# Reading the expert tables in a step of their own, spreading the token turns to one a half, and moving the late expert tiles

## The chip, the cores and the metric

The kernel runs on one core of a Trainium2 chip. Time is device microseconds (us) of one execution; the figure to be explained is the median of several. One execution was also taken with the hardware profiler; it has a time of its own, which differs a little from the median.

The core has five engines that work side by side, each with its own instruction queue: TensorE (PE in the profile, PEld for its weight loads), VectorE (DVE), ScalarE (ACT), GpSimd (POOL) and SyncE (SP). DMAs are issued from an engine's queue and land later.

## The reference, cut to what matters

```
x                                   # 4 batches x 2048 tokens x 512
xn  = layernorm(x)
q,k,v = split(xn @ w_qkv)           # 16 heads of 32
q,k = spectral_filter(q), spectral_filter(k)   # rfft, mask, irfft along the 32
out = softmax(q k^T / sqrt(32)) v @ w_out + b_out
moe: best = argmax(softmax(xn @ w_gate))       # 8 experts, top 1
     the first 100 tokens of each expert, in order over all 8192 tokens:
     gate * (xn @ w_expert + b_expert), else 0  # one w_expert for all
return x + out + moe
```

At most 800 tokens get an expert's output. They are the 800 *slots*, kept as 7 tiles of 128 rows, called expert rows 0 to 6 here.

## The kernel before, in words

**Groups, blocks, windows, halves.** Everything is float32. The work is cut into 16 *groups*, each one batch with 4 of its 16 heads (`k`; batch `k // 4`, head group `c = k % 4`). A group has four *blocks* of 512 queries (`n`). A block goes over 16 key tiles of 128 (`j`). One key tile of one block is a *half*; a *window* is two halves, an even and an odd one. Halves are numbered through the program, 0 to 1023, 64 to a group and 16 to a block; a window is named here by its first half ("window 824").

In a half, TensorE computes the scores of 4 heads (keys x queries, 512 columns), and, between them, two *maxima* products of a block 21 halves ahead (queries x keys; VectorE reduces them, `part<-array`, to row maxima, which must be known before the exponentials, because the softmax subtracts them). ScalarE takes the exponentials of the scores into a tile of 128 x 2048 called `even` or `odd`, in two instructions of 1024 columns (`even<-array`, `odd<-array`). TensorE multiplies the tile of the half before with `v`, and VectorE adds that to `num`. After an even and an odd half, the odd tile is added onto the even one by an accumulating DMA of 1 MB from GpSimd's queue (`pair`: `even<-odd`), issued one window later; two windows later GpSimd adds the last window's even tile to this one in two instructions of 128 x 1024 (`add_to`, here "the sums": `even<-even`). So one even tile collects a block's denominators. There are five buffers for `even` and three for `odd`; an exponential waits when its buffer isn't free.

**Closing a block.** `close_steps(k, n)` lists the steps for the block that ended last, by halves after its end: *fold* (5: row sums by a product with ones), *invert* (6 to 13: eight reciprocals of 64 columns on VectorE), *divide* (on GpSimd, at the 14th half), *result* (17 to 20: the output projection of 128 tokens each, copied to `y`), *add* (21: `out_dram<-y`, an accumulating DMA of 1 MB from GpSimd's queue). For the last block but one (`(k, n) == (15, 2)`) they lie closer: fold at 5, inverts at 6 to 8, divide at 9, results from 10, add at 14.

**Pieces.** The keys, queries and values of the next group are computed in the halves of this one, in *pieces* of 128 tokens. There are three kinds: QK with `s = 0`, QK with `s = 1`, and V. Each piece has a first and a last half (`release`, `stop`), and a small planner, `level`, puts each in a half that has little cost yet. "QK3.3" is the last 128 tokens of the fourth 512.

**Turning groups.** Groups 3, 7 and 11 are the last of their batch; there the next batch's tokens are prepared. For each of the 16 token tiles, ScalarE *normalises* it (`normalize`, in the half before, in place), and TensorE *turns* it (`turn`: four transposes, then ScalarE copies the result to `xnT`). `TURNS` says in which half of the group each tile is turned; a piece can only be computed behind the turn of its own tile. Later in the same group the tokens' experts are found (`follow_route`), and each token's number and gate are sent by indirect DMAs to four tables of slots (`table<-entry,slot`). In the last batch the same is done in group 11, and the tables are read in group 12, the first group of the last batch.

**Expert rows.** `expert_steps` has the steps and `place_experts` their halves, written out by hand:

- `begin` (half 804): loads of `w_expert` and `b_expert`, the loads of the four tables (`entries<-table`, SyncE's queue), the reduction of these to one (`entry`, `who`: two VectorE reductions and a copy), a GpSimd memset of the first row buffer;
- `clear_rest`: the memset of the second one;
- `fetch(i)`: gathers row tile `i` from `x` by an indirect DMA from GpSimd's queue;
- `measure(i)`: mean and variance of the row tile on VectorE;
- `scale`: for all seven rows together, GpSimd computes `rstd` and `shift`;
- `expert(i)`: ScalarE normalises row `i` with `rstd` and `shift` (`xg<-xg,shift,rstd`); in the same step row `i-1` is turned and row `i-2` multiplied with the weights, for rows 0 to 3;
- for rows 4 to 6, the *late tiles*, `turn_row` and four `expert_columns` (128 output columns each) are placed in the last group by `LATE`: the first number of each tuple is the half of the turn, the others the halves of the columns, counted from half 960;
- `gather_row(i)`, `add_row(i)`, `scatter_row(i)`, two halves apart: gather the rows from the output by an indirect DMA, add on GpSimd, and scatter them back by an indirect DMA. All of them, and `out_dram<-y`, write to or read the same output and so wait for the landing of the one before.

**What sets the order.** Nothing reorders at run time: VectorE, ScalarE, GpSimd and TensorE are kept in program order (`InOrder`, whose line 83 records every operation, so all rows of the profile name L83). In a window the order is: the split of the maxima, the steps in `heads` (divide), `pair`, `add_to`, then for each of the two halves the scores, maxima, exponentials and their reductions, the product with `v`, and last `agenda[half]` with all steps placed there (steps placed by `behind` come last). An engine that stands before an instruction holds all that is behind it.

PSUM has eight banks. Banks 0 to 3 hold the scores; class `Oldest` hands out 4 to 7 for the maxima and for everything else that needs one.

Of the kernel before, what the change touches and what calls it, by code (L numbers as in the profile page):

```python
# [12 lines left out]
F32 = mybir.dt.float32  # L13
# [8 lines left out]
B, S, DM = 4, 2048, 512  # L22
# [3 lines left out]
P = 128  # L26
NT = S // P
NR = DM // P
# [4 lines left out]
TQ = QB // P  # L33
SLOTS = E * CAP
ST = -(-SLOTS // P)
EARLY = 4
LATE = ((14, 15, 16, 22, 23), (24, 25, 26, 27, 28), (29, 30, 31, 32, 38))
NTAB = 4
FAR = 1 << 20
EPS = 1e-5  # L40
# [62 lines left out]
def attention_and_top1_experts(ctx: ExitStack, tc: tile.TileContext, a: dict, out: bass.AP):  # L103
# [56 lines left out]
    small = ctx.enter_context(tc.tile_pool(name="small", bufs=1))  # L160

    def chunk(name):
        tag, bufs = ("y", 1) if name == "y" else ("xs", None)
        return chunks.tile([P, TQ, DM], F32, tag=tag, name=name, bufs=bufs)
# [28 lines left out]
    on = SimpleNamespace()  # L193
# [367 lines left out]
    def expert_steps():  # L561


        def begin():
            w_exp = chunk("w_exp")
            on.sync.dma_start(out=w_exp, in_=a["L0_ffn_w_expert"].rearrange("(r p) n -> p r n", p=P))
            b_exp = work.tile([P, DM], F32, tag="b_exp", name="b_exp", bufs=1)
            on.sync.dma_start(out=b_exp, in_=a["L0_ffn_b_expert"].partition_broadcast(P))
            entries = small.tile([P, NTAB, ST, 2], F32, name="entries")
            for i, table in enumerate(tables):  # L570
                on.sync.dma_start(out=entries[:, i], in_=table.rearrange("(t p) c -> p t c", p=P))
            entry = small.tile([P, ST, 2], F32, name="entry1")
            for i, op in enumerate((ALU.min, ALU.max)):
                on.vector.tensor_reduce(
                    entry[:, :, i], entries[:, :, :, i].rearrange("p n t -> p t n"), AX.X, op
                )
            who = small.tile([P, ST], I32, name="who")
            on.vector.tensor_copy(who, entry[:, :, 0])
            xg = [chunk("xg"), small.tile([P, ST - TQ, DM], F32, name="xg1")]
            on.gpsimd.memset(xg[0], 0.0)  # L580
            mv = small.tile([P, ST, 2], F32, name="mv1")
            index = [bass.IndirectOffsetOnAxis(ap=who[:, i : i + 1], axis=0) for i in range(ST)]
            bound = {"bounds_check": B * S - 1, "oob_is_err": False}
            taken.update(mv=mv, w_exp=w_exp, b_exp=b_exp, entry=entry, index=index, bound=bound, xg=xg)

        def clear_rest():
            on.gpsimd.memset(taken["xg"][1], 0.0)

        def row(i):
            return taken["xg"][i // TQ][:, i % TQ, :]  # L590

        def fetch(i):
            on.gpsimd.indirect_dma_start(row(i), None, rows, taken["index"][i], **taken["bound"])

        def measure(i):
            stats = small.tile([P, 6], F32, name="stats1")
            on.vector.bn_stats(stats, row(i))
            on.vector.bn_aggr(taken["mv"][:, i, :], stats)

        def scale():  # L600
            rstd = small.tile([P, ST], F32, name="rstd1")
            on.gpsimd.tensor_scalar(rstd, taken["mv"][:, :, 1], EPS, None, ALU.add)
            on.gpsimd.tensor_tensor(rstd, rstd, power[:, 0:ST], ALU.pow)
            shift = small.tile([P, ST], F32, name="shift1")
            on.gpsimd.tensor_tensor(shift, taken["mv"][:, :, 0], rstd, ALU.mult)
            on.gpsimd.tensor_scalar(shift, shift, -1.0, None, ALU.mult)
            taken.update(rstd=rstd, shift=shift)

        def turn_row(i):
            px = bank()  # L610
            for r in range(NR):
                on.tensor.transpose(px[:, r * P : (r + 1) * P], row(i)[:, r * P : (r + 1) * P], ident)
            taken["xt"] = work.tile([P, QB], F32, tag="byx", name="xt", bufs=1)
            on.scalar.copy(taken["xt"], px)

        def expert_columns(i, q):
            cols = slice(q * P, (q + 1) * P)
            pe = bank()[:, cols]
            for r in range(NR):
                columns(  # L620
                    pe,
                    taken["xt"][:, r * P : (r + 1) * P],
                    taken["w_exp"][:, r, cols],
                    start=(r == 0),
                    stop=(r == NR - 1),
                )
            on.vector.tensor_tensor(row(i)[:, cols], pe, taken["b_exp"][:, cols], ALU.add)
            if q == NR - 1:
                on.scalar.activation(row(i), row(i), AF.Copy, scale=taken["entry"][:, i : i + 1, 1])

        def expert(i):

            if 2 <= i < EARLY + 2:
                at = slice(i - 2, i - 1)
                pe = bank()
                for r in range(NR):
                    on.tensor.matmul(
                        pe,
                        lhsT=taken["xt"][:, r * P : (r + 1) * P],
                        rhs=taken["w_exp"][:, r, :],  # L640
                        start=(r == 0),
                        stop=(r == NR - 1),
                    )
                on.vector.tensor_tensor(row(i - 2), pe, taken["b_exp"], ALU.add)
            if 1 <= i <= EARLY:
                turn_row(i - 1)
            if 2 <= i < EARLY + 2:
                on.scalar.activation(row(i - 2), row(i - 2), AF.Copy, scale=taken["entry"][:, at, 1])
            if i < ST:
                at = slice(i, i + 1)  # L650
                on.scalar.activation(
                    row(i), row(i), AF.Identity, bias=taken["shift"][:, at], scale=taken["rstd"][:, at]
                )

        return clear_rest, begin, fetch, measure, scale, expert, turn_row, expert_columns

    def gather_row(i):
        if i < EARLY:
# [290 lines left out]
    def at(half, step, *args, cost=0):  # L949
        agenda[half].append(lambda: step(*args))  # L950
        costs[half] += cost
# [73 lines left out]
    def place_experts(start):  # L1025


        clear_rest, begin, fetch, measure, scale, expert, turn_row, expert_columns = expert_steps()
        first = start + 36
        at(first, begin)  # L1030
        at(first + 5, clear_rest)
        for i in range(ST):
            at(first + 2 + 2 * i, fetch, i)
            at(start + (46, 47, 48, 53, 55, 56, 57)[i], measure, i)
        at(first + 22, scale)
        for i in range(ST):
            at(first + 26 + 2 * i, expert, i, cost=(NR if 2 <= i < EARLY + 2 else 0) + (1 if 1 <= i <= EARLY else 0))
        tail = start + 3 * GH
        for i, (turned, *places) in enumerate(LATE):
            at(tail + turned, turn_row, EARLY + i, cost=0.5)  # L1040
            for q, half in enumerate(places):
                at(tail + half, expert_columns, EARLY + i, q, cost=1)
        for i in range(ST):
            free = start + GH + i * HB + 26 if i < EARLY else tail + (25, 30, 39)[i - EARLY]
            for step in (gather_row, add_row, scatter_row):
                at(free, step, i)
                free += 2

    def plan(k):
# [43 lines left out]
        for s in range(3):  # L1093
            mine = [piece for piece, kind in zip(pieces, kinds) if kind == s]
            for i, piece in enumerate(mine):
                n = i // TQ
                if s == 0:
                    stop = start + GH - MAX_AHEAD // 2 - 1 + n * HB
                    release = start + 1 + n * HB
                elif s == 1:  # L1100
                    release = start + SPENT + n * TQ
                    stop = release + 3 * TQ - 2
                else:
                    release, stop = start + 1, start + GH + i - 2
                if c == NG - 2 and b + 1 < B:
                    stop = min(stop, start + GH - (8 if s == 2 else 1))
                release = max(release, turned.get(i, start - 1) + 1)
                load = None
                if i == NT - 1 and k + 2 < B * NG:
                    load = lambda s=s: load_qkv_weights(k + 2, s)  # L1110
                jobs[s].append((release, stop, 0 if i else 5 + (k < 2), piece, load))
        for n in range(NQ):
            at(start + GH - 10 + n * TQ, key_steps, n)

    TURNS = (2, 4, 6, 6, 6, 7, 7, 8, 12, 12, 12, 13, 16, 19, 21, 22)
    SPENT = GH - HB - MAX_AHEAD // 2 + TQ
    ROUTE = len(first_route)
    assert ROUTE == 12 + NT + 1
# [174 lines left out]
```

## Time and profile before

| | |
|---|---|
| median of 3 runs | 4135.46 us (4131.81 to 4139.23) |
| profiled execution, its own time | 4130.4 us |
| its span in the profile | 4128.6 us |
| TensorE (PE) busy | 4105.5 us, 99% of the span |
| VectorE (DVE) busy | 3418.3 us, 83% |
| GpSimd (POOL) busy | 3015.6 us, 73% |
| ScalarE (ACT) busy | 2486.1 us, 60% |
| DMAs issued by software (GpSimd's) | 601.63 MB, 74.7% of 16 DMA engines |
| `even<-odd`, 1 MB each | 504, median 8.3 us from issue to landing |
| `out_dram<-y`, 1 MB each | 63, median 9.9 us from issue to landing |

The span is the stretch that the profiler saw; the 1.8 us beyond it lie around the program. A row of a group or timeline names the engine, the operation and `out<-in` by the program's names, with the shape as partitions x elements; behind the bar, or in brackets, stands the idle time of the engine just before and what ended it. In a table by windows each cell is the busy time with its number of instructions, for PE, PEld, DVE, ACT, POOL and SP in turn; behind them the granted clock of TensorE (1.00 is full speed), the share of the DMA engines, and what they moved in GB/s.

Share of busy time in 40 slices of the span, in tenths:

```profile
PE   9999999999999999999999999999999999999999
DVE  7888887978888888797888888888788888888885
ACT  4555565676655556567665556566666555665665
POOL 1678776776887777676787766767678777786787
```

### The profile page before, as it was taken

To read this page: it belongs to the slowest core of one execution; us is meant where nothing else is said; L and a number is where in the kernel's file an instruction comes from. 1 tells how busy PE (TensorE), PEld (TensorE's weight loads), DVE (VectorE), ACT (ScalarE), POOL (GpSimd) and SP (SyncE) were. 2 spreads that over 40 slices of the span, in tenths; PEclk is the share of its full clock that TensorE was granted. 3 is DMA by queue.
4 is the path that set the end of the run, shared out by engine and by line. 5 is a ranking of instruction groups with operands and counts; after the bars stand their busy time and mean duration, and the time that the engine had idled before them with its cause. 6 is when DMAs were issued, how large, how long until landed. Compare 5 with 4: busy or idle time off the path is not lost.

```text
span 4128.6 us, 122052 instructions
## 1 busy us (share of the span) xinstructions
PE 4105.5 (99%) x53184; PEld 1832.0 (44%) x53184; DVE 3418.3 (83%) x4876; ACT 2486.1 (60%) x3424; POOL 3015.6 (73%) x2122
## 2 busy tenths in 40 slices
PE   9999999999999999999999999999999999999999
PEld 5444445444444444444444444444444444444442
DVE  7888887978888888797888888888788888888885
ACT  4555565676655556567665556566666555665665
POOL 1678776776887777676787766767678777786787
PEclk9999999999999999999999999999999999999999
DMA  4787887987788878899788788789887887877877
GB/s 127 147 165 154 160 165 160 226 186 147 154 161 162 163 155 161 188 203 193 145 158 160 158 161 160 159 191 208 171 160 151 173 163 150 170 163 156 163 152 147
DMA packets 179488, 680.81 MB, mean 165 GB/s; under 512 B 23478, under 2 KB 54360, under 8 KB 114184
## 3 DMA queue, kind: packets, MB, share of 16 engines
q0 software_dynamic: 109856, 601.63, 74.7%
q1 hardware_dynamic: 69024, 71.34, 5.3%
q8 instruction: 416, 6.82, 0.6%
q14 instruction: 120, 0.98, 0.1%
q10 hardware_dynamic: 72, 0.03, 0.0%
HBM read 71.07 MB, written 87.91 MB: 39 GB/s over the span
## 4 chain that ended last, share of the span: by engine, by line
PE 97%; DVE 1%; DMA 1%; POOL 0%; issue 0%; ACT 0%; SPq 0%; POOLq 0%; ACTq 0%; DVEq 0%
PE array L83 97%; DVE part L83 1%; POOL even L83 0%; DMA even<-odd 0%; DMA entries<-table 0%; DMA odd<-in_L_attn_w_qkv_dram 0%; ACT xs L83 0%; DVE num L83 0%; ACT xnT L83 0%; DVE factor L83 0%; DMA table<-entry,slot 0%; DVE stats L83 0%; POOL out_dram L83 0%; ACT odd L83 0%; POOL rest L83 0%
## 5 line engine op out<-in xcount | busy, mean ns | idle before, releaser
L83 DVE TENSOR_REDUCE part<-array 128x1 f32<-128x512 f32 (+1 forms) x3066 | 2480.7, 865 | 630.4 <-PE array L83 625.4
L83 POOL TENSOR_TENSOR even<-even 128x1024 f32<-128x1024 f32 x876 | 2123.9, 2527 | 466.7 <-DMA even<-odd 465.8
L83 PE MATMUL array<-keys,q 32*128 32x512 f32 x8192 | 2040.9, 613 | 2.5 <-ACT keys L83 0.8
L83 PE MATMUL array<-q,steps_of_keys 32*128 32x512 f32 x8128 | 2009.7, 614 | 0.2
L83 ACT ACTIVATE odd<-array 128x1024 f32<-128x1024 f32 x1024 | 994.7, 1021 | 462.5 <-PE array L83 388.0
L83 ACT ACTIVATE even<-array 128x1024 f32<-128x1024 f32 x1014 | 983.7, 1021 | 417.8 <-PE array L83 409.5
L83 PEld LDWEIGHTS array<-keys,q 32*128 32x128 f32 x8192 | 760.1, 184 | 540.7 <-DVE part L83 326.7
L83 PEld LDWEIGHTS array<-q,steps_of_keys 32*128 32x128 f32 x8128 | 690.4, 183 | 243.4 <-issue 227.0
L83 DVE TENSOR_TENSOR num<-num,array 128x512 f32<-128x512 f32 x960 | 651.0, 678 | 37.7 <-PE array L83 37.7
L83 POOL DMA_DIRECT2D even<-odd x504 | 462.4, 917 | 277.1 <-ACT odd L83 235.6
L83 PEld LDWEIGHTS array<-xnT,w 128*32 128x32 f32 x16384 | 460.0, 110 | 286.3 <-DVE part L83 196.0
L83 PE MATMUL array<-odd,v 128*32 128x512 f32 x4096 | 546.3, 605 | 0.5 <-DVE part L83 0.5
L83 PE MATMUL array<-even,v 128*32 128x512 f32 x4056 | 540.1, 605 | 3.3 <-DVE part L83 3.3
L83 PE MATMUL array<-xnT,w 128*32 128x128 f32 x16384 | 534.7, 273 | 1.1 <-ACT xnT L83 1.0
L83 PEld LDWEIGHTS array<-w,xnT 128*32 128x32 f32 x8192 | 231.5, 110 | 144.6 <-DVE part L83 100.3
L83 DVE RECIPROCAL factor<-den 128x64 f32<-128x64 f32 x504 | 274.7, 546 | 0.0
L83 PE MATMUL array<-w,xnT 128*32 128x128 f32 x8192 | 267.9, 273 | 0.1
L83 PE MATMUL array<-wo,ot 128*32 128x512 f32 x2048 | 266.7, 593 | 0.0
L83 PEld LDWEIGHTS array<-odd,v 128*32 128x32 f32 x4096 | 80.7, 108 | 388.6 <-DVE part L83 380.6
L83 PEld LDWEIGHTS array<-even,v 128*32 128x32 f32 x4056 | 79.8, 108 | 387.9 <-DVE part L83 383.4
L83 POOL DMA_DIRECT2D out_dram<-y x63 | 87.4, 1387 | 156.3 <-ACT y L83 112.1
L83 ACT COPY keys<-array 128x128 f32<-128x128 f32 x256 | 68.2, 266 | 176.8 <-PE array L83 172.3
(152 smaller groups left out, 1540.5 us busy)
## 6 DMA issues: line engine op xcount, KB each, us to landing
even<-odd POOLq DMA_DIRECT2D x504, 1024.0 KB, 8.3
out_dram<-y POOLq DMA_DIRECT2D x63, 1024.0 KB, 9.9
xs<-in_L_attn_x_dram SPq DMA_DIRECT2D x96, 256.0 KB
out_dram<-in_L_attn_x_dram SPq DMA_DIRECT2D x16, 1024.0 KB
w<-wd SPq DMA_DIRECT2D x30, 256.0 KB
w<-in_L_attn_w_qkv_dram SPq DMA_DIRECT2D x16, 256.0 KB
wo<-in_L_attn_w_out_dram SPq DMA_DIRECT2D x16, 256.0 KB
negm<-row SPq DMA_DIRECT2D x192, 4.0 KB
```

The source lines that it names most:

```text
L83: done = act(*args, **kwargs)
```

## The change

Three things are changed, all in where steps stand; no instruction is added or removed.

1. *Turns.* `TURNS` no longer has two or three turns in one half; each of the 16 tiles has a half of its own. The last half allowed for the QK pieces of the group ahead of a turning group goes from the last half of that group (`start + GH - 1`) to the first half of the turning group (`start + GH`). By the planner, the one piece that this moves there is QK3.3, from half 191 to half 192 (and alike in the two other turning groups); the pieces that wait for a turn move with the turns.
2. *Tables.* The reduction of the tables is taken out of `begin` into a step of its own, `read_tables`, five halves behind it. The steps behind it move: fetches from halves 806, 808, ... 818 to 810, 811, 813, 814, 816, 817, 819; measures from 814, 815, 816, 821, 823, 824, 825 to 814, 816, 821, 823, 825, 827, 829; `clear_rest` from 809 to 806; `scale` from 826 to 830; `expert(i)` from 830 + 2i to 831 + 2i.
3. *Late tiles.* The turns of rows 4, 5, 6 move from halves 974, 984, 989 to 973, 982, 987; their columns to the halves right behind these, but for row 4's last one, which moves to 982; the last columns of row 6 from half 998 to 991. The gather, sum and scatter go from 985, 987, 989 to 984, 986, 988 (row 4), from 990, 992, 994 to 988, 990, 992 (row 5), and from 999, 1001, 1003 to 993, 995, 997 (row 6). The last of these, `scatter_row(6)`, now stands in half 997, right behind the `out_dram<-y` of the block that ended at half 976.

```diff
-LATE = ((14, 15, 16, 22, 23), (24, 25, 26, 27, 28), (29, 30, 31, 32, 38))
+LATE = ((13, 14, 15, 16, 22), (22, 23, 24, 25, 26), (27, 28, 29, 30, 31))
...
             for i, table in enumerate(tables):
                 on.sync.dma_start(out=entries[:, i], in_=table.rearrange("(t p) c -> p t c", p=P))
+            xg = [chunk("xg"), small.tile([P, ST - TQ, DM], F32, name="xg1")]
+            on.gpsimd.memset(xg[0], 0.0)
+            mv = small.tile([P, ST, 2], F32, name="mv1")
+            taken.update(mv=mv, w_exp=w_exp, b_exp=b_exp, entries=entries, xg=xg)
+
+        def read_tables():
+            entries = taken["entries"]
             entry = small.tile([P, ST, 2], F32, name="entry1")
             for i, op in enumerate((ALU.min, ALU.max)):
                 on.vector.tensor_reduce(
...
             who = small.tile([P, ST], I32, name="who")
             on.vector.tensor_copy(who, entry[:, :, 0])
-            xg = [chunk("xg"), small.tile([P, ST - TQ, DM], F32, name="xg1")]
-            on.gpsimd.memset(xg[0], 0.0)
-            mv = small.tile([P, ST, 2], F32, name="mv1")
...
         first = start + 36
         at(first, begin)
-        at(first + 5, clear_rest)
+        at(first + 2, clear_rest)
+        at(first + 5, read_tables)
         for i in range(ST):
-            at(first + 2 + 2 * i, fetch, i)
-            at(start + (46, 47, 48, 53, 55, 56, 57)[i], measure, i)
-        at(first + 22, scale)
+            at(first + 6 + 3 * i // 2, fetch, i)
+            at(start + (46, 48, 53, 55, 57, 59, 61)[i], measure, i)
+        at(first + 26, scale)
         for i in range(ST):
-            at(first + 26 + 2 * i, expert, i, cost=...)
+            at(first + 27 + 2 * i, expert, i, cost=...)
...
-            free = start + GH + i * HB + 26 if i < EARLY else tail + (25, 30, 39)[i - EARLY]
+            free = start + GH + i * HB + 26 if i < EARLY else tail + (24, 28, 33)[i - EARLY]
...
                 if c == NG - 2 and b + 1 < B:
-                    stop = min(stop, start + GH - (8 if s == 2 else 1))
+                    stop = min(stop, start + GH - (8 if s == 2 else 0))
...
-    TURNS = (2, 4, 6, 6, 6, 7, 7, 8, 12, 12, 12, 13, 16, 19, 21, 22)
+    TURNS = (2, 4, 6, 7, 8, 9, 10, 12, 13, 14, 15, 16, 18, 20, 21, 22)
```

More of the change, by code (lines that the diff above doesn't have):

```diff
@@ L578, in begin @@
             on.vector.tensor_copy(who, entry[:, :, 0])
-            xg = [chunk("xg"), small.tile([P, ST - TQ, DM], F32, name="xg1")]
-            on.gpsimd.memset(xg[0], 0.0)
-            mv = small.tile([P, ST, 2], F32, name="mv1")
             index = [bass.IndirectOffsetOnAxis(ap=who[:, i : i + 1], axis=0) for i in range(ST)]
             bound = {"bounds_check": B * S - 1, "oob_is_err": False}
-            taken.update(mv=mv, w_exp=w_exp, b_exp=b_exp, entry=entry, index=index, bound=bound, xg=xg)
+            taken.update(entry=entry, index=index, bound=bound)
         def clear_rest():
@@ L653, in expert @@
                 )
-        return clear_rest, begin, fetch, measure, scale, expert, turn_row, expert_columns
+        return begin, clear_rest, read_tables, fetch, measure, scale, expert, turn_row, expert_columns
     def gather_row(i):
@@ L1025, in place_experts @@
     def place_experts(start):
-        clear_rest, begin, fetch, measure, scale, expert, turn_row, expert_columns = expert_steps()
+        begin, clear_rest, read_tables, fetch, measure, scale, expert, turn_row, expert_columns = expert_steps()
         first = start + 36
         at(first, begin)
-        at(first + 5, clear_rest)
+        at(first + 2, clear_rest)
+        at(first + 5, read_tables)
         for i in range(ST):
-            at(first + 2 + 2 * i, fetch, i)
-            at(start + (46, 47, 48, 53, 55, 56, 57)[i], measure, i)
-        at(first + 22, scale)
+            at(first + 6 + 3 * i // 2, fetch, i)
+            at(start + (46, 48, 53, 55, 57, 59, 61)[i], measure, i)
+        at(first + 26, scale)
         for i in range(ST):
-            at(first + 26 + 2 * i, expert, i, cost=(NR if 2 <= i < EARLY + 2 else 0) + (1 if 1 <= i <= EARLY else 0))
+            at(first + 27 + 2 * i, expert, i, cost=(NR if 2 <= i < EARLY + 2 else 0) + (1 if 1 <= i <= EARLY else 0))
         tail = start + 3 * GH
```

## The prediction

> **What bounds the kernel.** First the page's head and its shares of the chain that ended last.
>
> ```profile
> span 4128.6 us, 122052 instructions
> ...
> PE 97%; DVE 1%; DMA 1%; POOL 0%; issue 0%; ACT 0%; SPq 0%; POOLq 0%; ACTq 0%; DVEq 0%
> ```
>
> TensorE is the bound, and the change removes no matmul, so only waits of TensorE can come or go. To find them I cut the trace into halves: matmuls stand in program order, a float32 matmul leaves two records and a transpose one, so counting records gives each half's first matmul, and a half lasts from its start to the next. A half without a step takes 2.91 us, a projection piece or a result adds 0.88, a turned tile 0.59; nearly all halves fit. What is over that is a wait.
>
> Next the chain in order of time, at the expert tables, and the granted clock by windows.
>
> ```profile
> 3260.72 2.17 DMA table<-entry,slot
> ...
> 3262.90 7.88 DMA entries<-table
> ...
> 3272.03 68.20 PE array L83 x858
> ```
>
> ```profile
> 3266.79:3273.88 7.09, 4.03 (x36) 1.31 (x32) 3.90 (x9) 1.98 (x2) 4.75 (x5) 1.00 1.09 187
> ...
> 4072.80:4076.20 3.40, 3.40 (x18) 0.59 (x16) 0.69 (x1) 1.99 (x3) 0.77 (x1) 0.50 1.02 274
> ```
>
> VectorE stands before the reduction of the tables until they land, and the maxima behind it hold TensorE: half 805 takes 7.09 us, where its like take 3.94. The column after POOL is the clock: 1.00 over that gap (3.06 us idle), 0.50 for 3.4 us late in the last block.
>
> Then the timelines of GpSimd, where the steps of the change queue, and of ScalarE, which waits for it: start, duration, instruction, and in brackets the idle time before it and what ended that.
>
> ```profile
> 3351.81 4.68 POOL L83 TENSOR_TENSOR even<-even 128x1024 f32<-128x1024 f32 x2 [3.92 <-DMA even<-odd]
> 3356.44 0.85 POOL L83 DMA_DIRECT2D even<-odd  x1
> 3357.03 4.96 POOL L83 TENSOR_TENSOR even<-even 128x1024 f32<-128x1024 f32 x2
> 3362.09 0.26 POOL L83 TENSOR_SCALAR rstd<-mv 128x7 f32<-128x7 f32 x1
> ...
> 3364.33 0.28 POOL L83 TENSOR_SCALAR shift<-shift 128x7 f32<-128x7 f32 x1
> ...
> 4028.86 1.31 POOL L83 DMA_DIRECT2D out_dram<-y  x1 [1.59 <-ACT y L83]
> ...
> 4030.90 0.91 POOL L83 DMA_DIRECT2D even<-odd  x1
> 4034.53 4.67 POOL L83 TENSOR_TENSOR even<-even 128x1024 f32<-128x1024 f32 x2 [2.73 <-DMA even<-odd]
> 4040.78 1.10 POOL L83 DMA_INDIRECT w<-out_dram,who  x1 [1.58 <-DMA out_dram<-y]
> ```
>
> ```profile
> 3369.96 0.81 ACT L83 ACTIVATE xg<-xg,shift,rstd 128x512 f32<-128x512 f32 x1
> ...
> 4057.59 1.94 ACT L83 ACTIVATE even<-array 128x1024 f32<-128x1024 f32 x2 [1.14 <-POOL even L83]
> ...
> 4070.04 1.94 ACT L83 ACTIVATE odd<-array 128x1024 f32<-128x1024 f32 x2 [4.27 <-DMA even<-odd]
> ```
>
> GpSimd works far behind the program: `scale`, issued in half 826 (start 3351.09), ends at 3364.61, 13.5 us later. ScalarE's first use came at 3369.96, so that was free. At the end, exponentials wait for GpSimd's sums or its DMAs to give their buffers back.
>
> **The parts.** The sum is made against the profiled execution, 4130.4 us (span 4128.6), 5.1 under the median of 4135.46; the difference is carried to the median.
>
> *Turns.* In a turning group the waits over the fit are 0.52, 0.18, 0.18, 0.48, 0.63, 0.55, 0.18, 0.18 (halves 1, 3, 5, 7, 8, 13, 20, 22): 2.9 us. The 0.48, 0.63 and 0.55 follow halves in which two or three turns and as many normalisations queue on ScalarE. With one of each, ScalarE has 2.04 (exponentials) + 0.59 + 0.81 + 0.27 = 3.7 us of work in a half of 4.39, and the four halves that already hold one piece and one turn (8, 13, 16, 22) delay nothing behind them. The 0.52 follows a half 0 without a piece, and the last query piece now fills it. A turn beside a result or a fold still costs its 0.18, now five times: 0.9. Saved 2.0 a group, three groups: -6.0. The pieces moved by this cost the same 0.88 where they land, and weights still have five halves (19 us) to arrive.
>
> *Tables.* The reduction goes five halves on, to 809, about 18 us; the entries land at 3270.8, before it. 7.09 becomes 3.94: -3.15. The memset (1.40 us) and the fetches only change place on GpSimd; a fetch lands 3.4 to 4.6 us after its issue, and `measure` follows by four halves or more (15 us), so that even 10 us of lag on GpSimd is covered. The reduction's three instructions (0.2 us each, started 0.1 apart) end on VectorE before the next maxima are there: 0.
>
> *Measures.* One behind a reciprocal costs 0.33 (halves 824 to 826, at 4.11 to 4.13 instead of 3.80). Three become four, one of them with some slack: +0.15.
>
> *Scale and the first expert row.* `scale` goes from 826 to 830, but the row that needs it only from 830 to 831. In the changed kernel's order ScalarE has: exponentials of 831, row 0 (waits for the shift on GpSimd), the copy of piece V3.3, the exponentials of 832. On GpSimd I follow the rows: the sums of window 824 start 9.5 us into half 824, when their DMA lands (before: 3351.81, 9.0 in); then sums 4.7 twice, key step 1.2, split 1.5, sums 4.9, division 1.3, sums 4.7, `scale` 2.5, DMA issues and their waits 2, together 27.5. Half 830 starts 23.8 after half 824, so `scale` ends at 830 + 13.2. ScalarE reaches row 0 at 830 + 7.3 and stands 6 us. Behind it stands V3.3, whose bank the second maxima of half 832 need at 830 + 9.2; row 0 (0.8) and the copy (0.27) end at 14.2. TensorE waits 5.0 us. If GpSimd came 3 us sooner it would be 2, if 3 later 8. A gap of 2.31 us inside a stretch of 3.4 was followed by 0.50 for 3.4 us, while 3.06 us at the tables was not. 5 us lies beyond both, so I take one such stretch, 1.7 us (bounds 0 and 3.4): +6.7. The skill's "TensorE: Matmul & The Clock Gate", Part 1, has a free-running window of about 3.4 us, over which an idle array drops to half rate; by it the drop is nearly certain and the part is +6.7, and without any drop it is +5.0.
>
> *Expert rows.* Odd halves instead of even: a result drained late by VectorE now meets a turn (half 834, up to 0.8), other places swap: +0.6 (0 to 1.5).
>
> *Late tiles.* Their columns are drained by VectorE after a reciprocal, 0.17 each, more where a turn shares the half. Before 2.0 us over halves 973 to 997; after, more of them in halves with a reciprocal, and half 992 empty: 2.75. +0.75 (0 to 2).
>
> *The last scatter.* Each `scatter_row` and `gather_row` waits for the landing of the write to `out` before it, and GpSimd stands meanwhile. Before, `gather_row(6)` waited thus for `out_dram<-y`, with one DMA and two sums run in between (4030.90 to 4039.2). After, `gather_row(5)` and `gather_row(6)` stand right behind a scatter (1.7 us each, from its landing of 2.8), which with row 6's own gather and sum (2.4) makes GpSimd 5.5 us later by half 997; and `scatter_row(6)` stands right behind that `out_dram<-y`, whose landing took 11.7 us here and 13.5 at 3333.32, just behind another DMA, as it will be. From half 998's start: `out_dram<-y` issued at 2.0, landed 15.5, the DMA of window 998 issued at 17.3 (before: -0.2), sums of 998 done at 22.7. The exponential of 1002 needs that buffer at 14.6, so it waits 8. The queue then runs on DMA (7.6) and sums (4.7): windows 1000, 1002, 1004 issue at 23.3, 30.3, 37.4. Before, the last of these was at 29.3, and the two waits behind it (4070.04, 4075.82) hung on it. They come 8.1 later, with 0.88 less work in between, since row 6's last columns left half 998: +8.9. With the shorter landing it is +7; bounds +4 and +11. The skill's "DMA: Bandwidth & Descriptors", Anatomy of one DMA, gives 2.0 us + bytes/436e3, an estimate of 4.4 us for this 1 MB; by it GpSimd would stand 9 us less and this part be about 0, the whole sum -1. The rows of the same transfer, 11.7 and 13.5, go against it.
>
> Sum: -6.0 - 3.15 + 0.15 + 6.7 + 0.6 + 0.75 + 8.9 = +7.95. On the median 4143.4, on the profiled execution 4138.4. Its own range, with the bounds but not all at one end: 4137 to 4150.
>
> **Rivals.**
> 1. *GpSimd is early enough at both places*, because with its steps spread it no longer lags, so neither new wait reaches TensorE. For: exponentials have five even and three odd buffers, 8 to 15 us of cover, and row 6's work has left the end of the queue, which would bring the last DMA 2 us forward. Against: 13.5 us of lag at `scale`, and a wait written into the queue. -6.0 - 3.15 + 1.5 - 2 = -9.6: 4126. It decides if `scale` ends within 7 us of half 830.
> 2. *One of the two alone*: -1 or +1, 4135 to 4137.
> 3. *The lateness piles up*: GpSimd reaches both places some 3 us later than I reckon (the missing pause at 805 gives it 3.15 us less to catch up), and each stall drops the clock twice: +3 at `scale`, +1.7, +2 at the end, 4150.
> 4. *The turns save nothing*, if a half with piece, turn and normalisation is as slow as the present 8 and 13: then +14, in with the third.
>
> **Numbers.** The forecast lies at the edge of 0.2% (8.3 us, about what a measurement of this kernel can tell from no change); I give its upper side more, since a wait that empties TensorE makes others late and none of the bounds runs as far down. Forecast 0.55 (0.33 slower, 0.22 same), rival 2 0.11 (same), rivals 3 and 4 0.19 (slower), rival 1 0.15 (faster): faster 0.15, same 0.33, slower 0.52. 4128 to 4151 leaves out most of the first and the end of the third.
>
> **What would show it.** Right: half 805 at 3.9 us; no half of a turning group over its work by more than 0.2; `xg<-xg,shift,rstd` on ScalarE with a wait of about 6 us put down to GpSimd, and a gap of 5 on TensorE; the indirect `out_dram<-xg` behind the last but one `out_dram<-y` of GpSimd waiting some 12 us, then an `even<-array` waiting about 8. Wrong: `scale` done before 830 + 7, a scatter that waits under 4 us, or turning groups that keep their 2.9 us.

## The result and the profile after

The changed kernel takes 4143.49 us (median of 15 runs, 4141.23 to 4146.85), the kernel before beside it 4138.09: a ratio of 1.0017, with a 95% interval of 1.0011 to 1.0024. By that ratio it is 7 us slower (4.5 to 9.9), against the 8 that the prediction had; the two medians themselves lie 5.4 us apart. In a later set, beside another set of runs of the kernel before, it was 1.0023 (1.0014 to 1.0032).

The profiled execution took 4145.56 us, 15.2 more than the profiled one of before, which is more than twice what the ratio gives. The two profiles must therefore not simply be subtracted; where the rest comes from is shown further below. The head of the page and its shares of the chain of waits:

```profile
span 4143.8 us, 122054 instructions
...
PE 97%; POOL 1%; DMA 1%; DVE 0%; issue 0%; ACT 0%; SPq 0%; POOLq 0%; ACTq 0%
```

In the chain GpSimd (POOL) has come up from 0% to 1%, since waits for it have come, and VectorE (DVE) has gone from 1% to 0%. The shares are too coarse to show the wait for the tables, which was 3 us; the table below shows that it is gone. The two instructions more than before are not TensorE's: there are four more waits for semaphores and two fewer reductions of the maxima.

The table by windows, for half 805 first, and then for the two stretches in which TensorE's clock was halved (columns as before: PE, PEld, DVE, ACT, POOL, then the clock):

```profile
3269.03:3272.99 3.96, 3.96 (x36) 1.28 (x32) 3.79 (x6) 1.98 (x2) 3.36 (x4) 1.00 1.11 198
...
3378.60:3385.40 6.80, 5.14 (x42) 2.23 (x46) 1.92 (x2) 2.92 (x4) 6.69 (x6) 0.50 0.62 130
...
4061.25:4068.05 6.80, 4.13 (x16) 1.36 (x17) 0.00 (x0) 3.88 (x4) 6.74 (x5) 0.50 0.85 172
```

Half 805 lasts 3.96 us, with TensorE busy throughout. The two stretches at 0.50 lie in halves 832 and 1002 to 1003, the two places that the prediction named, and each is 6.8 us long.

At the first place, GpSimd's timeline, then ScalarE's:

```profile
3371.59 4.99 POOL L83 TENSOR_TENSOR even<-even 128x1024 f32<-128x1024 f32 x2
3376.67 0.26 POOL L83 TENSOR_SCALAR rstd<-mv 128x7 f32<-128x7 f32 x1
...
3378.92 0.29 POOL L83 TENSOR_SCALAR shift<-shift 128x7 f32<-128x7 f32 x1
```

```profile
3379.24 0.81 ACT L83 ACTIVATE xg<-xg,shift,rstd 128x512 f32<-128x512 f32 x1 [4.85 <-POOL shift L83]
```

Half 830, in which the program has `scale`, began at 3367.03. GpSimd finished it at 3379.21, 12.2 us later (13.2 had been reckoned), and expert row 0 on ScalarE stood 4.85 us for it (6 had been reckoned). Half 832 took 10.72 us instead of 3.9.

TensorE's timeline has a gap at each of the two places, at the first behind ScalarE's copy `v`, which stands behind row 0, and at the second behind the late exponential:

```profile
3380.26 1.22 PE L83 MATMUL array<-keys,q 32*128 32x512 f32 x1 [3.22 <-ACT v L83]
...
4063.92 2.99 PE L83 MATMUL array<-q,steps_of_keys 32*128 32x512 f32 x8 [6.85 <-ACT even L83]
```

At the second place, GpSimd and ScalarE again:

```profile
4040.96 1.23 POOL L83 DMA_DIRECT2D even<-odd  x1
4041.53 2.00 POOL L83 DMA_DIRECT2D out_dram<-y  x1
4055.45 1.09 POOL L83 DMA_INDIRECT out_dram<-xg,who  x1 [11.93 <-PE array L83]
...
4057.24 0.91 POOL L83 DMA_DIRECT2D even<-odd  x1
```

```profile
4062.84 1.94 ACT L83 ACTIVATE even<-array 128x1024 f32<-128x1024 f32 x2 [9.05 <-POOL even L83]
```

The last scatter stands 11.93 us behind `out_dram<-y`. The row puts this down to TensorE, which had been done with row 6 long before; the wait is one for several semaphores, and I read it as one for the landing of `out_dram<-y`, which the profile of before names at `w<-out_dram,who` behind the same transfer. The `even<-odd` of window 998 is issued at 4057.24, 16.8 us into half 998 (17.3 had been reckoned), and the exponential of half 1002 waits 9.05 us for its buffer. Half 1002 lasts 10.17 us. At the very end, in return, halves 1009 and 1010 fall from 5.54 and 5.47 us to 3.16 and 3.63, while 1011 and 1012 rise by 0.8 and 0.9.

### The profile page after: what moved, and what is told of

It reads as the page before. It is cut to its first block, busy times and chain, and to the rows that moved or that the text cites. A ratio compares the mean times of both kernels' runs of the same rounds, so it can differ in the third digit from the quotient of the medians.

```text
span 4143.8 us, 122054 instructions
## 1 busy us (share of the span) xinstructions
PE 4115.4 (99%) x53184; PEld 1837.6 (44%) x53184; DVE 3418.0 (82%) x4874; ACT 2491.3 (60%) x3424; POOL 3019.4 (73%) x2122
## 4 chain that ended last, share of the span: by engine, by line
PE 97%; POOL 1%; DMA 1%; DVE 0%; issue 0%; ACT 0%; SPq 0%; POOLq 0%; ACTq 0%
PE array L83 97%; POOL even L83 1%; DVE part L83 0%; DMA even<-odd 0%; DMA out_dram<-y 0%; DMA odd<-in_L_attn_w_qkv_dram 0%; ACT xs L83 0%; POOL ot L83 0%; POOL xnT L83 0%; ACT xnT L83 0%; POOL rstd L83 0%; POOL xg L83 0%; POOL rest L83 0%; POOL steps_of_keys L83 0%; POOL row L83 0%
## 5 line engine op out<-in xcount | busy, mean ns | idle before, releaser
L83 ACT COPY q<-array 128x128 f32<-128x128 f32 x256 | 68.4, 267 | 183.3 <-PE array L83 183.2
```

Source lines behind the costliest of these rows:

```text
L83: done = act(*args, **kwargs)
```

## Experiments

Times of a set are compared with the runs of the kernel before in the same set; its medians were 4135.64 us in the first set, 4131.73 in the second and 4131.50 in the third. "Over the fit" is what a half takes beyond its work, as in the prediction. Lengths of halves and groups are from the profiles.

### First set: is it the two waits, and why do the profiles lie so far apart?

**The kernel before, once more.**

> The kernel before, unchanged, for a second profile of it and the spread. Theory A (the change's time is TensorE's waits at four places: turning groups -5.2 us in the profiles, reduction of the tables -3.1, expert row 0 behind scale +6.1, last scatter behind out_dram<-y +9.5): ratio 1.000 within 0.0005, and the small waits that only the profile of the changed kernel had so far (ten halves in which ScalarE's first copy starts 0.7 to 1.0 us late, 3 us in all, half 800 longer by 1.0, the first half 1.15 later) turn up here too, in other halves: they vary from execution to execution, and are why the two profiles lie 15 us apart and the medians 5. Rival B (those small waits are made by the change): again none of them here, and a span near 4129.

Measured: ratio 0.9997 (0.9988 to 1.0006), span 4132.7 us. The small waits of the changed kernel's profile are here too. So they are not of the change, and Rival B falls. Something else turned up: half 805 lasts 3.96 us in this profile, with nothing to wait for. The table wait of the profile of before is not in every execution.

**`scale` two halves earlier.**

```diff
-            at(start + (46, 48, 53, 55, 57, 59, 61)[i], measure, i)
-        at(first + 26, scale)
+            at(start + (46, 48, 53, 55, 56, 57, 59)[i], measure, i)
+        at(first + 24, scale)
```

> The changed kernel with scale two halves earlier (828 instead of 830) and the last three measures at 824, 825, 827 so that they still stand ahead of it; expert row 0 stays in half 831. Theory A: scale then ends on GpSimd some 4 us before ScalarE comes to row 0, half 832 shrinks from 10.72 us to 3.9, with no clock of 0.50 behind it; the two measures in neighbouring halves cost 0.3 each: -6 us against the changed kernel, ratio to before 1.0002 (0.9995 to 1.0008). Rival B: the wait at row 0 goes, but the small late starts of ScalarE stay: the ratio is the same by that, but the profile still has some ten late copies where the control has none. Rival C (GpSimd's lag moves with its work, so that the sums stand later instead): half 832 shrinks, but an even exponential within ten halves waits for GpSimd, and less than 3 us are won: ratio over 1.0010.

Measured: 4140.24 us, ratio 1.0009 (1.0000 to 1.0018), against 1.0017 for the changed kernel. The last step of `scale` on GpSimd, and then row 0 on ScalarE:

```profile
3371.10 0.28 POOL L83 TENSOR_SCALAR shift<-shift 128x7 f32<-128x7 f32 x1
```

```profile
3375.26 0.81 ACT L83 ACTIVATE xg<-xg,shift,rstd 128x512 f32<-128x512 f32 x1
```

The shift is there 3.9 us ahead of row 0, whose row has no bracket any more; half 832 falls from 10.72 to 3.91 us, and no clock of 0.50 follows. That is the 6.8 us of this place. In the medians 3.3 of it appeared (4143.49 less 4140.24, of different sets), and the ratio's interval holds Theory A's 1.0002 as well as Rival C's 1.0010. What Rival C names isn't seen: in the ten halves behind row 0 no exponential waits for GpSimd. But this profile has 1.9 over the fit in half 812 and 0.9 in half 810, which the changed kernel's has not.

**The last scatter ahead of `out_dram<-y`.**

```diff
-            free = ... else tail + (24, 28, 33)[i - EARLY]
+            free = ... else tail + (24, 28, 32)[i - EARLY]
```

> The changed kernel with gather, sum and scatter of row 6 one half earlier (992, 994, 996): the last scatter then stands ahead of the out_dram<-y of half 997, not behind it. Theory A: its wait of 11.9 us on GpSimd goes; out_dram<-y waits some 2 us for the scatter's landing instead; the exponential of half 1002 waits under 2 us instead of 9, half 1002 is at most 4.5 us long (10.17 in the changed kernel) without the clock of 0.50, and the last group is 10 us shorter (7 to 13): ratio to before 0.9993 (0.9985 to 1.0002). Rival C (GpSimd is too far behind there anyhow, by the expert rows put before it): the wait moves to halves 1002 to 1012 and under 5 us are won: ratio over 1.0005.

Measured: 4143.55 us, ratio 1.0016 (1.0007 to 1.0026): nothing is won. GpSimd's timeline, and ScalarE's:

```profile
4041.93 1.10 POOL L83 DMA_INDIRECT out_dram<-xg,who  x1 [0.30 <-issue]
4049.18 1.32 POOL L83 DMA_DIRECT2D out_dram<-y  x1 [6.14 <-ACT even L83]
...
4050.69 1.43 POOL L83 DMA_DIRECT2D even<-odd  x1
```

```profile
4056.85 1.94 ACT L83 ACTIVATE even<-array 128x1024 f32<-128x1024 f32 x2 [3.61 <-POOL even L83]
4063.36 1.94 ACT L83 ACTIVATE odd<-array 128x1024 f32<-128x1024 f32 x2 [4.57 <-DMA even<-odd]
```

Now `out_dram<-y` stands 6.14 us behind the scatter, which itself was issued right behind an `even<-odd` of 1 MB. The row names ScalarE, which was done earlier; I read the wait as one for the scatter's landing. The next `even<-odd` then goes out right behind the 1 MB of `out_dram<-y`. The wait of 9 us becomes several smaller ones: halves 1002 to 1005 last 4.73, 6.51, 4.79 and 4.35 us. Theory A's account of this place is wrong: it is not that one wait which costs, for without it the lateness stands elsewhere. Rival C, that GpSimd is too far behind there anyhow, holds here.

**Both edits.**

> Both edits of the last two kernels at once: what is left of the change is the turns, the tables, and the late tiles without either queue wait. Theory A: the two gains add up, -16 us against the changed kernel, -9 against the one before (turns -5.2, tables -3.1, end -1): ratio 0.9978 (0.9970 to 0.9986). Rival B (the small late starts belong to the change): 3 to 5 us less won, ratio 0.9988 to 0.9992. Rival C: over 0.9993.

Measured: 4139.43 us, ratio 1.0008 (0.9999 to 1.0017). It is as the `scale` edit alone; halves 1002 to 1004 last 4.77, 6.44 and 4.72 us. Rival C again.

### Second set: each part alone on the kernel before

**The turns.** `TURNS` of the changed kernel and its `stop`, nothing else.

> The kernel before with the turns of the changed one (and the one piece moved to the turning group) alone. Theory D (three parts that add up: the turns win 1.8 us in each of three turning groups; the tables win nothing, because in the control half 805 has no wait and group 12 is as long as in the changed kernel; scale and the late tiles lose 7 each): -5.3 us, ratio 0.9987 (0.9981 to 0.9993), the over-fit waits of a turning group fall from 5.4 to 3.7. Rival E (what the turns win is lost again behind them, as slack that other waits take): groups 3, 7 and 11 shorter by 1.8 each, but the span as before, ratio over 0.9995.

Measured: 4125.21 us, ratio 0.9982 (0.9973 to 0.9991), 6.5 us faster. Each of the groups 3, 7 and 11 has 3.6 us over the fit, where the kernel before has 5.4. These 5.4 are the prediction's 2.9 and 2.5 more in half 24 of the group, where the product with `w_gate` stands and which is 6.36 us long in both kernels. Rival E falls. As an example, half 456 (half 8 of group 7), with one piece and one turn, in the kernel before and then with the turns alone (the first number behind the window is its length):

```profile
1888.20:1893.21 5.01, 5.01 (x62) 2.58 (x61) 3.95 (x6) 3.98 (x7) 4.30 (x3) 1.00 1.16 265
...
1887.25:1891.63 4.38, 4.38 (x61) 2.20 (x60) 3.47 (x6) 3.39 (x5) 2.00 (x2) 1.00 1.08 218
```

**The tables**, in the form without the wait at row 0 (`read_tables` at `first + 5`, `scale` at `first + 24`, rows from `first + 27`).

> The kernel before with the tables' part alone, in the form without the wait at row 0 (scale at 828, last measures at 824, 825, 827): reading the tables in half 809, fetches from 810, rows from 831. Theory D: half 805 at 3.96 us, but the cast of the token numbers on VectorE stands beside a sum on GpSimd and takes 0.4 to 1.7 us instead of 0.17, and ScalarE's copy of half 812 is late behind two fetches (1.8): group 12 within 1.5 us of the control's 251.1, ratio 1.0000 (0.9994 to 1.0006). Rival F (the 3.1 us of half 805 in the profile of before are what an execution has as a rule, and reading later wins them): ratio 0.9993 or less.

Measured: 4129.82 us, ratio 0.9996 (0.9987 to 1.0006): 1.9 us faster or nothing. The interval reaches Rival F's 0.9993, so F is neither carried nor excluded. Half 805 lasts 3.96 us, half 810, where the reduction now stands, 4.51 instead of 3.80. The late copy in half 812 did not come (3.80 us).

**The late tiles.** `LATE` and `free` of the changed kernel.

```diff
-LATE = ((14, 15, 16, 22, 23), (24, 25, 26, 27, 28), (29, 30, 31, 32, 38))
+LATE = ((13, 14, 15, 16, 22), (22, 23, 24, 25, 26), (27, 28, 29, 30, 31))
-            free = ... else tail + (25, 30, 39)[i - EARLY]
+            free = ... else tail + (24, 28, 33)[i - EARLY]
```

> The kernel before with the late tiles' halves alone. Theory D: GpSimd is some 5 us later at half 997 and stands 12 us before the scatter of row 6, as in the changed kernel: half 1002 at about 10 us, groups 14 and 15 together 6 to 7 us longer, ratio 1.0016 (1.0010 to 1.0022). Rival E (GpSimd's lateness in the last group comes from the tables' or turns' part, through the exponentials that stand later): half 1002 under 5 us, ratio under 1.0006.

Measured: 4140.86 us, ratio 1.0024 (1.0014 to 1.0034), 9.1 us slower, 2 to 3 more than Theory D had, about what the columns' halves turn out to cost further below. Half 1002 lasts 10.23 us. GpSimd's timeline:

```profile
4053.37 1.09 POOL L83 DMA_INDIRECT out_dram<-xg,who  x1 [11.95 <-PE array L83]
```

The scatter stands 11.95 us, as in the changed kernel. So this part brings its wait with it, without the other two, and Rival E falls.

**The turns, and row 6's steps behind the block's last sums.** This is no part of the change, but its opposite: the gather, sum and scatter of row 6 go later.

```diff
-            free = ... else tail + (25, 30, 39)[i - EARLY]
+            free = ... else tail + (25, 30, 48)[i - EARLY]
```

> The kernel before with the turns, and with gather, sum and scatter of row 6 nine halves later (1008, 1010, 1012), behind the last sums of the block. Theory D: GpSimd's queue then holds no wait for a landing between half 997 and the last accumulating DMA; that DMA is issued 5 us earlier, and the waits of halves 1009 and 1010 (5.54 and 5.47 us long instead of 2.9) shrink by 4 us together: -9 us with the turns, ratio 0.9978 (0.9970 to 0.9985). Rival G (the last DMAs are bound by the DMA engines, not by the queue): halves 1009 and 1010 as before, only the turns' gain, ratio 0.9987. If the gather at half 1008 stands before the outstanding DMA of the block instead: halves 1011 to 1020 longer by up to 5 us, ratio 0.999 or more.

Measured: 4122.39 us, ratio 0.9977 (0.9968 to 0.9986), 9.3 us faster than before, and faster than the turns alone by 2.8. The table by windows for halves 1009 and 1010:

```profile
4059.58:4062.74 3.16, 3.16 (x29) 0.96 (x25) 0.69 (x1) 2.91 (x5) 3.16 (x3) 1.00 1.02 207
4062.74:4065.66 2.92, 2.92 (x28) 0.72 (x24) 1.34 (x2) 1.87 (x2) 2.75 (x2) 1.00 0.47 95
```

They take 6.1 us together instead of 11.0, TensorE is busy in all of it, and the clock stays at 1.00. Rival G falls. Of the 4.9 us, 3.0 come back in halves 1018 to 1020 (4.08, 4.03 and 3.83 us, with the turns alone 3.11, 2.92 and 2.93), and 0.5 more are saved in half 1008; the last group is 2.5 us shorter than with the turns alone (223.2 us against 225.7). GpSimd's timeline names the wait of a write behind a scatter here:

```profile
4074.02 1.08 POOL L83 DMA_INDIRECT out_dram<-xg,who  x1 [0.16 <-POOL xnT L83]
4077.00 1.37 POOL L83 DMA_DIRECT2D out_dram<-y  x1 [1.90 <-DMA out_dram<-xg,who]
```

With no transfer ahead of the scatter it is 1.90 us, where it was 6.14.

### Third set: do the parts add up, and columns against queue

**Turns, tables without the wait, row 6 late.**

> The kernel before with the turns, the tables in the form without the wait at row 0 (scale at 828), and row 6's gather, sum and scatter at 1008, 1010, 1012; the late columns as before. Theory D (the parts add up): turns -5.9 (between their 5.3 in the profiles and 6.5 in the medians), tables -1.9, row 6 -2.9: -10.7 us, ratio 0.9974 (0.9966 to 0.9981). Rival H (half 805's wait, won by reading the tables later, is taken up by the next wait down the queue, GpSimd's sums): as the turns and row 6 alone, ratio 0.9978 or more.

Measured: 4122.76 us, ratio 0.9977 (0.9967 to 0.9986). That is the ratio of the turns and row 6 alone (0.9977), so the tables' part adds nothing that can be told. It lies within Theory D's range and just under Rival H's bound, and doesn't decide between them. In the profiles half 805 is at 3.96 us instead of 5.42 in the profile without the tables' part, but half 810 at 4.54 instead of 3.80 and half 1020 at 5.29 instead of 3.83.

**The changed kernel with both queue waits mended**: `scale` at `first + 24` as above, and

```diff
-            free = ... else tail + (24, 28, 33)[i - EARLY]
+            free = ... else tail + (25, 30, 48)[i - EARLY]
```

> The changed kernel with scale at 828 (last measures at 824, 825, 827) and the gathers, sums and scatters of rows 4 and 5 where they were before and row 6's at 1008, 1010, 1012; turns, tables and the halves of the late tiles' turns and columns as in the changed kernel. Theory D (what the late part lost was GpSimd standing for landings, not the columns): within 2 us of the last kernel, ratio to before 0.9976 (0.9968 to 0.9984), half 1002 under 3.5 us. Rival I (the columns' halves are to blame, through VectorE and ScalarE): 5 us or more behind the last kernel, ratio 0.9986 or more.

Measured: 4122.89 us, ratio 0.9980 (0.9971 to 0.9989), half 1002 at 3.25 us, and within 0.2 us of the kernel before this one, whose columns are in the old halves. With these lines the changed kernel turns from 9.6 us slower (the last run of this set) to 8.6 faster. The edit spaces rows 4 and 5 as before and also moves row 6 out of the way; which of the two it needs, no run separates.

**The columns alone**: `LATE` of the changed kernel, `free` of before.

> The kernel before with the turns and columns of the late tiles in the changed kernel's halves, and their gathers, sums and scatters where they were. Theory D: the prediction's price for the columns, +0.75 us (0 to 2): ratio 1.0002 (0.9998 to 1.0006). Rival I: +5 us or more, ratio 1.0012 or more.

Measured: 4135.02 us, ratio 1.0007 (0.9998 to 1.0016): between Theory D and Rival I, 3.5 us by the medians, 2.4 in the last three groups of the profile (739.2 us against 736.9). Of this, 1.0 is in half 1010, which waits for the last `even<-odd`. Where row 6's steps are out of the way, as in the kernel above, nothing of it is left.

**The changed kernel, once more.**

> The changed kernel once more, beside the others and on their chip. Theory D: the four parts measured apart add up: turns -5.9, tables -1.9, scale two halves too late +6.1, late part +9.1 (the kernel with that part alone): +7.4 us, ratio 1.0018 (1.0010 to 1.0025); in its profile half 832 at 8 to 11 us, half 1002 near 10. Rival J (the parts hide each other): under +4 or over +11 us.

Measured: 4141.06 us, ratio 1.0023 (1.0014 to 1.0032), 9.6 us; half 832 at 11.69 us and half 1002 at 10.17. The sum of the parts was 7.4. They add up within what can be told.

## Why the prediction was right, term by term

| term | predicted, us | measured, us | by |
|---|---|---|---|
| turns | -6.0 | -6.5 | turns alone; 1.9 less over the fit in each of three groups |
| tables | -3.15 | -1.9 (may be 0) | tables alone |
| measures | +0.15 | +0.05 | halves 823 to 830, second profile of the changed kernel less before |
| scale and row 0 | +6.7 | +6.8 (3.3 by the medians of two sets) | half 832, 10.72 to 3.91 |
| expert rows | +0.6 | +0.15 | group 13 over the fit, 16.35 to 16.5, in the tables alone |
| late columns | +0.75 | +3.5 (2.4 in the profile) | columns alone |
| last scatter | +8.9 | +5.6 (7.2 in the profiles) | late part less columns alone |
| sum | +7.95 | +7 and +9.6 (the rows above: +7.7) | changed kernel, two sets |

The mechanism held at both places: a lagging GpSimd that ScalarE comes to wait for at row 0, and a write to the output that it stands for at the end. Both were found by adding GpSimd's rows in order and setting the sum against the time at which ScalarE comes by; both lags came out within about 1 us, and that decided between the forecast and its first rival, in which GpSimd is early enough.

Four terms were mis-sized, and they cancel, so the closeness of the sum is in part luck. That the forecast of 4143.4 met the median of 4143.49 is luck too: the forecast was added to a median of before of 4135.46, and the kernel before took 4138.09 beside the changed one. The measured 0.17% lies just below the edge of 0.2% that the prediction drew between "same" (0.33) and "slower" (0.52), and the later 0.23% just above it.

*Tables.* The 7.09 us of half 805 were taken from one profile as what a run has. Six profiles that read the tables in the old place have 7.09, 3.96, 5.24, 8.29, 5.42 and 7.02 us; their mean is 6.2, and 2.2 over the 3.96 that it takes without a wait. Five halves later the reduction was priced at 0, since it ends "before the next maxima are there". Half 810 takes 3.84 to 5.14 us in the eight profiles that read there (mean 4.6), 0.8 over its 3.80. So the part is worth 1.4 and not 3.15, and the tables alone measured 1.9.

*Scale.* Its sum was right, its split was not: in the first profile TensorE stood 3.2 us, not 5.0, and the clock was at 0.50 for 6.8 us, not for one stretch of 3.4. The row above has 5.14 us of work in it, which at half speed lost 2.6. Together that is 5.8 of the 6.8; where the last 1.0 lies, the rows do not say. The page of the skill that the prediction weighed, "TensorE: Matmul & The Clock Gate", Part 1, has the windows of 3.4 us; that there are two of them, only the trace told. By free-running windows of that length a gap of 5 us holds a whole one in about half of the cases, an estimate from the page's figure, so "nearly certain" was too much. Nor do the runs follow a rule of one whole idle window, and they decide: a gap of 1.4 us went with a halved clock, and one of 3.06 with none (last section).

*Columns.* They were priced by VectorE's drains. In the profile of the columns alone, with a turn counted as 0.59 of work, halves 973 and 987, which took on a turn beside an inversion, have 0.3 to 0.4 us more over the fit, 983 behind such a half 0.6, and 993 and 999, behind the halves that lost their columns, 0.5 and 0.3; the halves that the turns left (974, 984, 989) give back 0.1 to 0.3 each. Some 1.4 us remain, and 1.0 in half 1010.

*Last scatter.* The step that failed is the reason, not the size: "`scatter_row(6)` stands right behind that `out_dram<-y`". Set ahead of it, it cost the same. (The price of that wait was right: the scatter starts 13.9 us after the issue of `out_dram<-y`, against the 13.5 taken from the rows and the 4.4 of the estimate that the prediction set against them.) The other half of the step stands: with the rows' gathers and scatters this close GpSimd is 4.5 us later at half 997 (`out_dram<-y` issued 6.0 us into its half instead of 1.5; 5.5 had been reckoned), and the accumulating DMAs behind are late whichever write to the output comes first. The mended kernel, where rows 4 and 5 are spaced as before and row 6 is out of the way, has none of it.

The profiles differ by 15.2 us, the runs by 7. Some 4 of these are explained: the profile of before has none of the late copies on ScalarE that the control and the changed kernel's first profile have (last section), and its execution is among the quickest of the kernel. Like beside like, the spans differ by 11.1 us (control 4132.7 and changed kernel 4143.8, both with late copies) and 10.7 (4128.6 and 4139.3, both without). That is still over the 7 of the first set and the 9.6 of the last; how long half 805 takes in the unprofiled runs isn't known.

## What to carry to other kernels

Where an engine runs behind its program, a step's place in the program says little about its time: add up that engine's rows in order from a known landing, and compare with the moment its reader comes by; two halves of room for `scale` were worth 6.8 us. In a queue in which each write waits for the landing of the one before, spread the writes and put the last ones where the engine idles, as the mended kernel does; swapping two of them only moves the wait. A wait seen in one profile may be a draw: take a second profile of the kernel before, and price the wait by its mean.

## What was not expected of the hardware

**A small cast on VectorE beside a sum on GpSimd.** VectorE's timeline of the kernel with both edits of the first set:

```profile
3288.13 1.72 DVE L83 CAST who<-entry 128x7 int32<-128x7 f32 x1
```

GpSimd's timeline there:

```profile
3285.14 4.67 POOL L83 TENSOR_TENSOR even<-even 128x1024 f32<-128x1024 f32 x2 [3.13 <-DMA even<-odd]
```

The same cast of 128 x 7 takes 0.17 us in the profiles of before and of the control, in half 805. In the eight profiles that have it in half 810 it takes 0.41 to 1.72 us, and in each of them it ends within 0.1 us of the end of one of GpSimd's sums: here at 3289.85, the sums at 3289.81. The two reductions just before it stay at 0.12 to 0.19 us, with the same sum running. The Trainium skill's page "SBUF — State Buffer", section "Who interferes with whom", has VectorE's casts, but not its reductions, among the instructions that can need the pair of ports shared with GpSimd, and lets the later one wait for the whole instruction of the other; the rows agree with that. The prediction's 0 for the three instructions was short of it by 0.8 us on average.

**ScalarE's copies beside the issue of an indirect DMA.** GpSimd's timeline of the control, and ScalarE's:

```profile
3183.84 1.07 POOL L83 DMA_INDIRECT table<-entry,slot  x1 [0.17 <-issue]
```

```profile
3185.21 0.27 ACT L83 COPY v<-array 128x128 f32<-128x128 f32 x1 [1.68 <-PE array L83]
```

Half 783 begins at 3184.07, and the copy of its piece is due 0.14 us later. It starts 1.0 us late, 0.3 us after the indirect DMA has been issued. In this profile 20 of 24 copies that fell due during such an issue were 0.2 to 1.0 us late. In the first profile of before none of 22 was, and none in the eight profiles of the second and third sets; in all of the first set and in the changed kernel's first one many were. So it belongs to the conditions of a set, not to the kernel, and it goes with the medians of the kernel before: 4138.09 and 4135.64 us with such copies in the profiles beside them, 4131.73 and 4131.50 without. The three sets of runs also had a different chip each, which no run separates from the rest of their conditions. What sets it stays open.

**The halved clock comes in pieces of 3.41 us, and the gap's length does not set them alone.** A gap of 1.4 us of TensorE in half 832 (the scatter edit of the first set) went with one such piece, gaps of 3.2 and 4.3 us there (the changed kernel's two profiles) with two, and two gaps of 1.4 and 1.9 us within 8 us of each other with four. The 3.06 us in half 805 of the kernel before went with none, and one of 2.69 us there, in the kernel with the late tiles alone, with one.
